# A two-layer metaformer in float32: the first state of each scan chunk, the last inverse transforms, and where VectorE's reductions stand

## The chip, the cores and the metric

The kernel runs on one core of one Trainium2 chip, in one launch. The metric is the device time of that launch in microseconds (us), and the median of several runs is compared. PE is the tensor engine, DVE the vector engine, ACT the scalar engine, POOL GpSimd, and SP the engine whose queue issues nearly all DMAs here.

## The reference, cut to what matters

The input is `x[4, 64, 64, 128]`: four images of 4096 tokens with 128 channels, all in float32. Layer 0 is a selective scan in four directions (`K = 4`, 256 inner channels, 16 states) and a mixture of 64 experts; layer 1 is a sum over rows and columns and a long convolution with 16 spectral filters. The parts that the change touches:

```python
def step(h, xs):                      # layer 0, conv: 4096 steps for each batch and direction
    ut, dt, bt, ct = xs
    dA = jnp.exp(dt[..., None] * A)
    h = dA * h + (dt * ut)[..., None] * bt[:, :, None, :]
    y = jnp.einsum('bkdn,bkn->bkd', h, ct)
    return (h, y)
...
logits = jnp.einsum('bsd,ed->bse', x, gate_w) + gate_b        # layer 0, experts
probs = jax.nn.softmax(logits, axis=1)                        # over the 4096 tokens
vals, idx = jax.lax.top_k(probs.transpose(0, 2, 1), K)
...
message_m = jnp.sum(inputs, axis=2)                           # layer 1, conv
message_k = jnp.sum(inputs, axis=1)
...
Uf_p = jnp.fft.rfft(u, n=n, axis=1)                           # layer 1, filters
U_plus = jnp.fft.irfft(Vf[None, :, :, None] * Uf_p[:, :, None, :], n=n, axis=1)[:, :sl]
...
x = x + _L1_conv_ref(_ln_c(x), ...)
t = _to_tokens(x)
t = t + _L1_ffn_ref(_ln_t(t), ...)
```

## The kernel before, in words

**The scan loop.** The main loop (`for s in range(-5, total + 2)`) walks over 2048 steps: 4 batches, 4 directions, 8 chunks of 512 tokens (`SC`), 16 states each. One step does one state of one chunk, for 2 x 128 channels and 512 tokens, on all engines, each at its own distance. SP loads `bc` (the rows B and C of that state, spread over 128 partitions) five steps ahead, L1435. ACT computes `da = exp(delta * A)` three steps ahead in two halves, L1445. DVE multiplies `db = du * B` into PSUM (L1473) and runs two scans `h = da * h + db` (L1479), one for each half of the channels. POOL stores the last column for the next chunk (`hst`, L1488) and multiplies by C one step behind (L1489). PE transposes and sums into `y` two steps behind, L1515. There are six `hh` buffers and five `da`; `db`, `du` and `y` have one PSUM buffer each.

**delta*x.** `step_sizes` prepares the next chunk in pieces, one a step: `dts` is projected, ACT and POOL make the softplus `dl`, and the last piece is POOL's product `dx = dl * xc` (L1377), in SBUF with one buffer. At state 15 of a chunk `into_psum` has ACT copy `dx` to `du` in PSUM in two halves (L1426). Every `db` of the next chunk reads `du`, the first one included.

**Side work.** The rest of the network is dealt between the scan's instructions: `beside(b)` is a generator whose pieces give their weight, and `deal` draws pieces until as much weight is made as is due. `WEIGHT` holds the total weight of each batch's side work, and so the pace. [...] a side instruction stands in its engine's queue between those of the scan. `pipelined(n, *stages)` staggers the stages of a piece of work: in each step the latest stage is written first, and a `None` is a step's distance. `LAG` (5.0) is a pause.

**Maxima and row sums.** `experts_and_sums` norms the tokens, transposes them (`turn`), and projects the gate's logits on PE (`logits`); ACT moves them to `pT` (L742), and DVE takes the maximum of each group of 512 tokens (L756), as the next stage of the same pipeline. Later, in the same manner, ACT (through `evict`, L257) writes transposed tokens to `xT`, DVE sums their rows (`mm`, L969), and then their columns (`mk`, L976).

**The tail.** After the scans, `side["tail"]` is set and eight PSUM banks are open. `convolve` runs the filters' matmuls (L1166, L1187) for the groups of frequencies that are left; a second generator runs beside it, first the last batch's experts and sums, then `back()`, the inverse transforms of batches 1 and 2. `ratio` sets how much filter work is drawn for each unit of it. PE's order is fixed by dependencies that `behind` adds. Last comes `from_slots(B - 1)`: it loads the products of the filters (`zb`, L1246) and the residual tokens (`xr` from `x3_d`, L1252), multiplies by the inverse transform on PE (`gi_ps`, L1259), scales on ACT (`iv`, L1261), adds on POOL (L1269) and stores (L1272), eight groups in a pipeline of five stages. Batch 0's inverse transforms run earlier, beside the scans of the last batch.

Of the kernel before, what the change touches and what calls it, by code (L numbers as in the profile page):

```python
# [10 lines left out]
F32 = mybir.dt.float32  # L11
# [20 lines left out]


FIRST = 1
WEIGHT = (1346.0, 2070.0, 1989.0, 2042.0)

BUSY = (2, 3)

# [40 lines left out]
def kernel(  # L79
# [137 lines left out]
    def evict_soon(work):  # L217
        if side["deals"]:
            soon.append(work)
        else:  # L220
            work()
# [113 lines left out]
    def transposed(dst, src, n, name):  # L335

        ps = bank([P, n, P], name)
        for q in range(n):
            nc.tensor.transpose(ps[:, q, :], src[:, q, :], ident)
        evict_soon(lambda: evict(dst, ps.rearrange("c q p -> c (q p)")))  # L340
# [374 lines left out]
    def experts_and_sums(b):  # L715

        with tc.tile_pool(name="mk", bufs=1) as kp:
# [3 lines left out]
            with tc.tile_pool(name="ga", bufs=2) as gp:  # L721
                tt = gp.tile([P, NBLK, C], F32, name="tt", bufs=1)
                mx8 = gp.tile([E, 8], F32, name="mx8", bufs=1)
                st, tT = {}, {}

                def t4(g):
                    return tt[:, 4 * g : 4 * g + 4, :]

                def gs(g):
                    return slice(512 * g, 512 * (g + 1))  # L730

                def sums(g):
                    st[g] = norm_sums(gp, t4(g), 4, C, eps5)

                def turn(g):
                    tT[g] = gp.tile([P, 512], F32, name="tT")
                    transposed(tT[g], t4(g), 4, "tt_ps")

                def logits(g):
                    ps = bank([E, 512], "lg_ps")  # L740
                    nc.tensor.matmul(ps, gw, tT[g], start=True, stop=True)
                    nc.scalar.activation(pT[:, gs(g)], ps, AF.Identity, bias=gb)  # L742

                yield from pipelined(
                    8,
                    (0.4, lambda g: nc.sync.dma_start(t4(g), tiles(x1_d[b], g))),
                    (3.0, sums),
                    (1.2, lambda g: norm_refine(gp, st[g], 4, C, 1e-5)),
                    None,
                    (1.2, lambda g: norm_apply(t4(g), t4(g), st[g], 4)),  # L750
                    None,
                    (1.0, turn),
                    (1.0, logits),
                    (
                        0.6,
                        lambda g: nc.vector.reduce_max(  # L756
                            mx8[:, g : g + 1], pT[:, gs(g)], axis=AX.X
                        ),
                    ),
                )  # L760

                nmx = gp.tile([E, 1], F32, name="nmx", bufs=1)
                nc.vector.reduce_max(nmx, mx8, axis=AX.X)
                nc.vector.tensor_scalar(nmx, nmx, -1.0, None, ALU.mult)
                s8 = gp.tile([E, 8], F32, name="s8", bufs=1)
                for g in range(8):
                    nc.scalar.activation(
                        pT[:, gs(g)], pT[:, gs(g)], AF.Exp, bias=nmx, accum_out=s8[:, g : g + 1]
                    )
                    yield 0.8  # L770
                yield LAG
                ssum = gp.tile([E, 1], F32, name="ssum", bufs=1)
                nc.vector.reduce_sum(ssum, s8, axis=AX.X)
                nc.vector.reciprocal(ssum, ssum)
                yield 1.0
                for g in range(8):
                    nc.scalar.activation(pT[:, gs(g)], pT[:, gs(g)], AF.Identity, scale=ssum)
                    yield 0.8
                yield LAG
                top = gp.tile([E, TOPK], F32, name="top", bufs=1)  # L780
                nc.vector.max(top, pT)
                yield 1.0
                rest = gp.tile([E, L], F32, name="rest", bufs=1)
                nc.vector.match_replace(rest, top, pT, 0.0)
                yield 1.0
                for g in range(8):
                    nc.gpsimd.tensor_sub(pT[:, gs(g)], pT[:, gs(g)], rest[:, gs(g)])
                    yield 1.2
                yield LAG
                po = bank([P, E], "po_ps")  # L790
                pk = {}

                def turn_back(g):
                    ps = bank([P, 8, E], "pk_ps")
                    for q in range(8):
                        t0 = (8 * g + q) * P
                        nc.tensor.transpose(ps[:, q, :], pT[:, t0 : t0 + P], ident[0:E, 0:E])
                    pk[g] = gp.tile([P, 8, E], F32, name="pk")
                    evict(pk[g], ps)

                def pool(g):
                    for q in range(8):
                        nc.tensor.matmul(
                            po,
                            tt[:, 8 * g + q, :],
                            pk[g][:, q, :],
                            start=(g == 0 and q == 0),
                            stop=(g == 3 and q == 7),
                        )

                yield from pipelined(4, (1.5, turn_back), (3.0, pool))
                evict(pooled, po)
                yield 1.0
                yield LAG
# [106 lines left out]
            with tc.tile_pool(name="l1", bufs=2) as lp:  # L921
# [4 lines left out]
                with tc.tile_pool(name="l1a", bufs=2) as la:  # L926
# [25 lines left out]
                    def apply(g):  # L952
# [11 lines left out]
                        (1.2, apply),  # L964
                        None,
                        (1.0, lambda g: transposed(xT[:, gs(g)], xn[g], 4, "xn_ps")),
                        (
                            0.6,
                            lambda g: nc.vector.reduce_sum(  # L969
# [3 lines left out]
                            ),  # L973
                        ),
                    )
                nc.vector.reduce_sum(  # L976
                    mk[:, 0, :], xT.rearrange("p (r w) -> p w r", w=W), axis=AX.X
                )
# [254 lines left out]

    def from_slots(b):

        with tc.tile_pool(name="gi", bufs=3) as gp:
            zb, xr, iv = {}, {}, {}

            def here(g):
                t0 = 2 * (BS - 4 * (g + 1))  # L1240
                return slice(t0, t0 + 8)

            def load(g):
                zb[g] = gp.tile([P, 4, 2, C], F32, name="zb")
                for r in range(2):
                    nc.sync.dma_start(  # L1246
                        zb[g][r * NQ : (r + 1) * NQ], zd[b][:, r, 4 * g : 4 * g + 4]
                    )

            def turn(g):  # L1250
                xr[g] = gp.tile([NB, 4, 2, C], F32, name="xr3", bufs=5)
                nc.sync.dma_start(  # L1252
                    xr[g].rearrange("j t a c -> j (t a) c"),
                    x3_d[b].rearrange("(j t) c -> j t c", j=NB)[:, here(g), :],
                )
                iv[g] = gp.tile([NB, 4, 2, C], F32, name="iv", bufs=4)
                for a in range(2):
                    ps = bank([NB, 4, C], "gi_ps")
                    nc.tensor.matmul(ps, gi_t, zb[g][:, :, a, :], start=True, stop=True)  # L1259
                    evict_soon(  # L1260
                        lambda ps=ps, a=a: nc.scalar.activation(  # L1261
                            iv[g][:, :, a, :], ps, AF.Identity, scale=wpj[0:NB, :]
                        )
                    )

            def add(g):

                for t in range(4):
                    nc.gpsimd.tensor_add(xr[g][:, t], xr[g][:, t], iv[g][:, 3 - t])  # L1269

            def put(g):
                nc.sync.dma_start(  # L1272
                    out[b].rearrange("(j t) c -> j t c", j=NB)[:, here(g), :],
                    xr[g].rearrange("j t a c -> j (t a) c"),
                )

            yield from pipelined(BS // 4, (0.7, load), (2.5, turn), None, (3.0, add), (0.5, put))

    def run(pieces):
        for _ in pieces:  # L1280
            tick()
        flush()
# [21 lines left out]
    with ExitStack() as c0:  # L1304
# [123 lines left out]
        for s in range(-5, total + 2):  # L1428
# [23 lines left out]
            if 0 <= s < total:  # L1452
# [17 lines left out]
                        next(sizes[i + 1][3], None)  # L1470
                hhs[s] = pb.tile([P, 2, SC], F32, name="hh", bufs=6)
                db = bps.tile([P, 2, SC], F32, name="db")
                nc.vector.tensor_mul(db, dus[i], bcs[s][:, 0:1, :].to_broadcast([P, 2, SC]))  # L1473
                for h in range(2):
                    init = 0.0 if step == 0 else hsts[i][:, h, n : n + 1]
                    o, d0, d1 = hhs[s][:, h, :], das[s][:, h, :], db[:, h, :]
# [76 lines left out]
    def first_stages():  # L1553
        yield from after_scans(B - 1)
        yield from experts_and_sums(B - 1)
        yield from to_slots(B - 1)

    def back():
        for b in range(1, B - 1):
            yield from from_slots(b)  # L1560

    last = len(all_groups) - NQ // 4
    with tc.tile_pool(name="cv_tail", bufs=2) as cp:

        for stages, groups, ratio in (
            (first_stages(), all_groups[BESIDE * (B - 1) : last], 3.2),
            (back(), all_groups[last:], 18.0),
        ):
            filtered = convolve(groups, cp)
            due = made = 0.0  # L1570
# [10 lines left out]
                start = len(traced)  # L1581
            run(filtered)
            behind(start, True)
    run(from_slots(B - 1))
    side["pool"].close()


# [72 lines left out]
```

## Time and profile before

| what | value |
|---|---|
| median of 3 runs | 11044.66 us (11032.29 to 11044.76) |
| the profiled execution | 11042.23 us, its span 11040.4 us, mean TensorE clock 0.864 |
| busy over the span | PE 79%, DVE 74%, ACT 57%, POOL 61% |
| L1489 POOL `hh<-hh,bc` | 2048 x 2358 ns |
| L1479 DVE `hh<-da,hst,db` (and `hh<-da,db`) | 3584 x 1267 ns (512 x 1208 ns) |
| L1473 DVE `db<-du,bc` | 2048 x 1232 ns |
| L1426 ACT `du<-dx` | 256 x 590 ns |
| L756 and L969 DVE `mx<-pT`, `mm<-xT` | 32 each, median 678 ns |
| L976 DVE `mk<-xT` | 4, median 7125 ns |
| L1261 ACT `iv<-gi_ps`, L1269 POOL `xr<-xr,iv` | 64 x 681 ns, 128 x 719 ns |

The times come from one profiled execution. Busy time counts only what an engine works on; a wait shows as idle time in front of an instruction, with the instruction that ended it named behind an arrow. The share of an engine over the whole span mixes stages with different limits, so the stages are read one by one. [...]

### The profile page before, as it was taken

The page shows a single profiled execution, that of the slowest core. Times are in us where ns is not written, and L with a number is a line of the kernel's source. Part 1 is how long each engine was busy: PE and PEld are TensorE (multiplying, and loading weights), DVE is VectorE, ACT ScalarE, POOL GpSimd, SP SyncE. Part 2 cuts the span into 40 slices and gives each one's busy share as a digit, 9 for nine tenths or more (in the row PEclk, how much of TensorE's full clock was granted, in tenths as well). Part 3 has the DMA queues.
Part 4 walks back from the last instruction along what each step waited for, and adds up shares of the span by engine and source line. Part 5 has one row for each costly group of instructions (what it writes and reads, how often), then busy time and mean ns, then how long its engine had stood idle before and what let it go on. Part 6 is the DMA issues. An engine that isn't in the chain of part 4 may idle for free. (4 is left out here: it accounts for less than half of the span.)

```text
span 11040.4 us, 119413 instructions
## 1 busy us (share of the span) xinstructions
PE 8697.3 (79%) x35936; PEld 4908.8 (44%) x35936; DVE 8146.2 (74%) x7046; ACT 6261.4 (57%) x12203; POOL 6771.4 (61%) x6198
## 2 busy tenths in 40 slices
PE   6787777657777777778776677687677789999999
PEld 2444444334464444445543334455344444355443
DVE  0888989987897999989988899798799922222222
ACT  4767676757567565675755556657565634134222
POOL 1777777877777878777777777677788711001001
PEclk9788888768887888878878888798888899999999
DMA  2455656657666666657565566475766664554555
GB/s 95 166 201 171 206 177 211 205 183 223 212 197 194 196 181 197 206 178 253 171 190 173 173 183 213 155 271 163 205 190 194 186 159 118 147 136 105 134 134 122
DMA packets 901466, 1980.29 MB, mean 179 GB/s; under 512 B 101562, under 2 KB 415578, under 8 KB 899290
## 3 DMA queue, kind: packets, MB, share of 16 engines
q1 hardware_dynamic: 900826, 1972.65, 59.2%
q8 instruction: 293, 4.80, 0.2%
q14 instruction: 347, 2.84, 0.1%
HBM read 1766.77 MB, written 205.52 MB: 179 GB/s over the span
## 5 line engine op out<-in xcount | busy, mean ns | idle before, releaser
L1489 POOL TENSOR_TENSOR hh<-hh,bc 128x1024 f32<-128x1024 f32 x2048 | 4827.9, 2358 | 419.5 <-DVE hh L1479 181.2
L1479 DVE TENSOR_TENSOR_SCAN hh<-da,hst,db 128x512 f32<-128x512 f32 x3584 | 4393.2, 1267 | 547.7 <-PE y L1515 165.7
L1445 ACT ACTIVATE da<-dl,aneg 128x512 f32<-128x512 f32 x4096 | 2773.3, 717 | 2018.1 <-DVE hh L1479 1946.7
L1515 PE MATMUL y<-ident,hh 128*128 128x128 f32 x16384 | 2655.8, 311 | 644.9 <-POOL hh L1489 538.5
L1515 PEld LDWEIGHTS y<-ident,hh 128*128 128x128 f32 x16384 | 2204.1, 161 | 2025.0 <-issue 1076.1
L1473 DVE TENSOR_TENSOR db<-du,bc 128x1024 f32<-128x1024 f32 x2048 | 2523.6, 1232 | 576.1 <-ACT du L1426 486.4
L1166 PE MATMUL cv_ps<-slab,us 64*128 64x512 f32 x4096 | 1169.4, 678 | 513.0 <-ACT y L257 276.5
L257 ACT COPY y<-cv_ps 128x512 f32<-128x512 f32 (+1 forms) x1024 | 754.9, 741 | 666.8 <-PE cv_ps L1166 636.6
L1488 POOL COPY hst<-hh 128x2 f32<-128x2 f32 x1792 | 336.4, 188 | 1237.8 <-DVE hh L1479 1111.3
L1187 PE MATMUL zq_ps<-y,me 128*128 128x512 f32 x2048 | 992.4, 604 | 44.8 <-ACT y L257 43.4
L1187 PE MATMUL zq_ps<-y,mo 128*128 128x512 f32 x2048 | 977.7, 601 | 0.0
L255 DVE COPY y<-cv_ps 128x512 f32<-128x512 f32 x640 | 441.9, 691 | 568.0 <-PE cv_ps L1166 550.3
L1166 PEld LDWEIGHTS cv_ps<-slab,us 64*128 64x128 f32 x4096 | 400.0, 203 | 963.1 <-ACT y L257 364.8
L1203 POOL TENSOR_TENSOR zt<-zt,zt 128x512 f32<-128x512 f32 x64 | 81.1, 1267 | 1082.7 <-DVE zt L255 571.4
L1479 DVE TENSOR_TENSOR_SCAN hh<-da,db 128x512 f32<-128x512 f32 x512 | 597.0, 1208 | 50.4 <-PE y L1515 14.0
L411 PE MATMUL cv_ps<-xh,diag 128*128 128x512 f32 x1152 | 529.1, 602 | 9.8 <-ACT dl L1370 6.9
L1187 PEld LDWEIGHTS zq_ps<-y,me 128*128 128x128 f32 x2048 | 348.7, 191 | 375.6 <-issue 261.3
L1187 PEld LDWEIGHTS zq_ps<-y,mo 128*128 128x128 f32 x2048 | 359.5, 192 | 317.1 <-issue 315.1
L1335 PE MATMUL dt_ps<-dts,dtw 8*128 8x512 f32 x512 | 336.0, 769 | 147.0 <-ACT sg_v L353 42.2
L255 DVE COPY zt<-zq_ps 128x512 f32<-128x512 f32 x40 | 27.7, 691 | 549.6 <-PE zq_ps L1187 549.6
L1361 POOL TENSOR_TENSOR ex<-ex,dx 128x1024 f32<-128x1024 f32 x128 | 302.4, 2363 | 159.3 <-ACT dx L1358 149.6
L317 POOL TENSOR_SCALAR no_a<-no_v 128x2 f32<-128x2 f32 (+1 forms) x224 | 43.0, 192 | 528.1 <-ACT no_sq L306 516.0
(232 smaller groups left out, 9290.4 us busy)
## 6 DMA issues: line engine op xcount, KB each, us to landing
bc<-bc_d SPq DMA_DIRECT2D x2048, 512.0 KB
slab<-hd SPq DMA_DIRECT2D x1024, 256.0 KB
xc<-xc_d SPq DMA_DIRECT2D x128, 512.0 KB
y_d<-ys SPq DMA_DIRECT2D x128, 512.0 KB
w1t<-in_w_dram SPq DMA_DIRECT2D x128, 512.0 KB
w2t<-in_w_dram SPq DMA_DIRECT2D x256, 256.0 KB
xc_x<-xc_d SPq DMA_DIRECT2D x64, 512.0 KB
yk<-y_d SPq DMA_DIRECT2D x128, 256.0 KB
```

The lines of the kernel that those rows point to most:

```text
L255: nc.vector.tensor_copy(dst, src)
L257: nc.scalar.copy(dst, src)
L411: nc.tensor.matmul(ps, diag[:, h, t, :], xh[:, 8 * g + dy : 8 * g + dy + 8, dx : dx + W], start=(t == 0), stop=(t == 8),)
L1166: nc.tensor.matmul(pq[q].rearrange("p (r k t) -> p r k t", r=2, t=BS), us[b, G][rows, p, a if e == 0 else 1 - a, :], slab[i][rows, p, :, : ...
L1187: nc.tensor.matmul(z, (me, mo)[e][:, KQ * kq + k, :], ys[e][:, :, :, :, k, :].rearrange("p a q r t -> p (a q r) t"), start=(e == 0 and k = ...
L1335: nc.tensor.matmul(ps, dtw[:, k, h * P : (h + 1) * P], dts, start=True, stop=True)
L1445: i_act = nc.scalar.activation(das[t][:, h, :], sizes[t // N][0][:, h, :], AF.Exp, scale=aneg[:, tk, h, t % N : t % N + 1],)
L1473: nc.vector.tensor_mul(db, dus[i], bcs[s][:, 0:1, :].to_broadcast([P, 2, SC]))
L1479: i_dve = nc.vector.tensor_tensor_scan(o, d0, d1, init, ALU.mult, ALU.add)
L1488: nc.gpsimd.tensor_copy(hsts[t // N][:, :, t % N], hhs[t][:, :, last])
L1489: i_pool = nc.gpsimd.tensor_mul(hhs[t], hhs[t], bcs.pop(t)[:, 1:2, :].to_broadcast([P, 2, SC]))
L1515: i_pe = nc.tensor.matmul(ys[c][:, q, h, :], hhs[t][:, h, q * P : (q + 1) * P], ident, is_transpose=True, start=(n == 0 and k > 0 and q % ...
```

## The change

Three edits, and two numbers that follow from them.

1. In the scan loop, the `db` of state 0 reads `dx` in SBUF (`sizes[i][1]`) in place of `du` in PSUM. The copies to `du` stay, and states 1 to 15 read `du`.
2. In `experts_and_sums`, a `None` stands in front of the maxima and in front of the row sums, and a `LAG` behind each of the two pipelines. `WEIGHT` of batches 1 to 3 grows by 10.
3. In the tail, `from_slots` has DVE read the inverse transform from PSUM, scale it and add the residual in one instruction (`scalar_tensor_tensor`) in place of ACT's scaling and POOL's addition; the stage in between and the addition's stage fall away, and the residual tokens (`load_x`) of all eight groups are loaded first, into eight buffers. For the last batch these loads are drawn at the end of `back()`, while the filters still run; the rest of it runs behind the filters as before. `ratio` of `back()` goes from 18 to 28.

```diff
--- before.py
+++ after.py
@@ -32,7 +32,7 @@
 
 
 FIRST = 1
-WEIGHT = (1346.0, 2070.0, 1989.0, 2042.0)
+WEIGHT = (1346.0, 2080.0, 1999.0, 2052.0)
 
 BUSY = (2, 3)
 
@@ -751,6 +751,7 @@
                     None,
                     (1.0, turn),
                     (1.0, logits),
+                    None,
                     (
                         0.6,
                         lambda g: nc.vector.reduce_max(
@@ -758,6 +759,7 @@
                         ),
                     ),
                 )
+                yield LAG
 
                 nmx = gp.tile([E, 1], F32, name="nmx", bufs=1)
                 nc.vector.reduce_max(nmx, mx8, axis=AX.X)
@@ -964,6 +966,7 @@
                         (1.2, apply),
                         None,
                         (1.0, lambda g: transposed(xT[:, gs(g)], xn[g], 4, "xn_ps")),
+                        None,
                         (
                             0.6,
                             lambda g: nc.vector.reduce_sum(
@@ -973,6 +976,7 @@
                             ),
                         ),
                     )
+                yield LAG
                 nc.vector.reduce_sum(
                     mk[:, 0, :], xT.rearrange("p (r w) -> p w r", w=W), axis=AX.X
                 )
@@ -1233,12 +1237,20 @@
 
     def from_slots(b):
 
-        with tc.tile_pool(name="gi", bufs=3) as gp:
+        tail = side["tail"]
+        with tc.tile_pool(name="gi", bufs=4 if tail else 3) as gp:
             zb, xr, iv = {}, {}, {}
 
             def here(g):
                 t0 = 2 * (BS - 4 * (g + 1))
                 return slice(t0, t0 + 8)
+
+            def load_x(g):
+                xr[g] = gp.tile([NB, 4, 2, C], F32, name="xr3", bufs=8 if tail else 5)
+                nc.sync.dma_start(
+                    xr[g].rearrange("j t a c -> j (t a) c"),
+                    x3_d[b].rearrange("(j t) c -> j t c", j=NB)[:, here(g), :],
+                )
 
             def load(g):
                 zb[g] = gp.tile([P, 4, 2, C], F32, name="zb")
@@ -1248,15 +1260,23 @@
                     )
 
             def turn(g):
-                xr[g] = gp.tile([NB, 4, 2, C], F32, name="xr3", bufs=5)
-                nc.sync.dma_start(
-                    xr[g].rearrange("j t a c -> j (t a) c"),
-                    x3_d[b].rearrange("(j t) c -> j t c", j=NB)[:, here(g), :],
-                )
-                iv[g] = gp.tile([NB, 4, 2, C], F32, name="iv", bufs=4)
+                if not tail:
+                    load_x(g)
+                    iv[g] = gp.tile([NB, 4, 2, C], F32, name="iv", bufs=4)
                 for a in range(2):
                     ps = bank([NB, 4, C], "gi_ps")
                     nc.tensor.matmul(ps, gi_t, zb[g][:, :, a, :], start=True, stop=True)
+                    if tail:
+
+                        nc.vector.scalar_tensor_tensor(
+                            xr[g][:, :, a, :],
+                            ps[:, ::-1, :],
+                            wpj[0:NB, :],
+                            xr[g][:, :, a, :],
+                            ALU.mult,
+                            ALU.add,
+                        )
+                        continue
                     evict_soon(
                         lambda ps=ps, a=a: nc.scalar.activation(
                             iv[g][:, :, a, :], ps, AF.Identity, scale=wpj[0:NB, :]
@@ -1274,6 +1294,12 @@
                     xr[g].rearrange("j t a c -> j (t a) c"),
                 )
 
+            if tail:
+                for g in range(BS // 4):
+                    load_x(g)
+                    yield 0.5
+                yield from pipelined(BS // 4, (0.7, load), (2.5, turn), (0.5, put))
+                return
             yield from pipelined(BS // 4, (0.7, load), (2.5, turn), None, (3.0, add), (0.5, put))
 
     def run(pieces):
@@ -1470,7 +1496,9 @@
                         next(sizes[i + 1][3], None)
                 hhs[s] = pb.tile([P, 2, SC], F32, name="hh", bufs=6)
                 db = bps.tile([P, 2, SC], F32, name="db")
-                nc.vector.tensor_mul(db, dus[i], bcs[s][:, 0:1, :].to_broadcast([P, 2, SC]))
+
+                src = sizes[i][1] if n == 0 else dus[i]
+                nc.vector.tensor_mul(db, src, bcs[s][:, 0:1, :].to_broadcast([P, 2, SC]))
                 for h in range(2):
                     init = 0.0 if step == 0 else hsts[i][:, h, n : n + 1]
                     o, d0, d1 = hhs[s][:, h, :], das[s][:, h, :], db[:, h, :]
@@ -1555,16 +1583,21 @@
         yield from experts_and_sums(B - 1)
         yield from to_slots(B - 1)
 
+    ends = from_slots(B - 1)
+
     def back():
         for b in range(1, B - 1):
             yield from from_slots(b)
 
+        for g in range(BS // 4):
+            yield next(ends)
+
     last = len(all_groups) - NQ // 4
     with tc.tile_pool(name="cv_tail", bufs=2) as cp:
 
         for stages, groups, ratio in (
             (first_stages(), all_groups[BESIDE * (B - 1) : last], 3.2),
-            (back(), all_groups[last:], 18.0),
+            (back(), all_groups[last:], 28.0),
         ):
             filtered = convolve(groups, cp)
             due = made = 0.0
@@ -1581,7 +1614,7 @@
                 start = len(traced)
             run(filtered)
             behind(start, True)
-    run(from_slots(B - 1))
+        run(ends)
     side["pool"].close()
```

## The prediction

> **What bounds the kernel now.** I read the page's slices first, then busy time by stretch, then VectorE's waits inside the first stretch. The slices show two regimes: VectorE (DVE) is nine tenths busy for 31 slices, then TensorE (PE) is.
>
> ```profile
> PE   6787777657777777778776677687677789999999
> DVE  0888989987897999989988899798799922222222
> ```
>
> The stretches (columns: length, then busy time and instructions of PE, weight loads, DVE, ACT, POOL, then clock and DMA) put the border at 8866 us:
>
> ```profile
> 297.00:8866.00 8569.00, 6374.86 (x28311) 3874.30 (x28312) 7599.45 (x6240) 5436.69 (x10260) 6510.21 (x5627) 0.83 0.62 194
> 8866.00:10995.00 2129.00, 2098.45 (x7139) 946.22 (x7137) 541.58 (x779) 678.98 (x1608) 201.89 (x458) 0.99 0.53 132
> 10995.00:11041.00 46.00, 20.71 (x36) 5.08 (x36) 0.69 (x1) 11.50 (x17) 23.22 (x33) 0.78 0.74 188
> ```
>
> Scan stage: 2048 steps in 8569 us, 4.18 us each, of which DVE works 3.71. Its 970 us of idle time is partly the short gap before each instruction; the rest are named waits, and only those can be saved. In the filter tail PE idles 31 us of 2129, so nothing on DVE, ACT or POOL pays there. The last 46 us are a chain of their own. DVE's waits in the scan stage (total, times, longest):
>
> ```profile
> DVE db L1473 <- ACT du L1426: 486.4, 57, 286.9
> DVE hh L1479 <- PE y L1515: 179.7, 55, 14.6
> DVE hh L1479 <- ACT da L1445: 66.9, 32, 7.4
> DVE mx L756 <- ACT pT L742: 54.1, 16, 6.6
> DVE mm L969 <- ACT xT L257: 19.3, 6, 5.5
> ```
>
> The 286.9 is the start-up, before the first scan. The other 56 waits on `du`, 199.5 us, fall at chunk starts: ACT's two copies of `dx` into PSUM stand behind side work in ACT's queue, and DVE waits for them. The last two lines are the maxima and row sums waiting for ACT's output.
>
> **What the Trainium skill says.** SBUF — State Buffer, Who interferes with whom: a VectorE instruction with two SBUF inputs contends with a GpSimd instruction that reads SBUF; the port is locked for the whole instruction and the later one blocks. That bears on the first part: `dx` and `bc` both lie in SBUF, `du` did not. The trace agrees. Timeline rows (start, length), from the few small two-input operations of the filter weights:
>
> ```profile
> 2277.16 0.15 DVE L631 TENSOR_TENSOR wt<-hard,soft 128x4 f32<-128x4 f32 x1
> 2277.52 2.35 POOL L1489 TENSOR_TENSOR hh<-hh,bc 128x1024 f32<-128x1024 f32 x1
> 2278.37 1.52 DVE L632 TENSOR_TENSOR wt<-wt,soft 128x4 f32<-128x4 f32 x1
> ...
> 2283.49 0.21 DVE L636 TENSOR_TENSOR wseg<-wseg,wt 128x1 f32<-128x1 f32 x1
> 2283.51 0.18 POOL L1488 COPY hst<-hh 128x2 f32<-128x2 f32 x1
> 2283.77 2.34 POOL L1489 TENSOR_TENSOR hh<-hh,bc 128x1024 f32<-128x1024 f32 x1
> ```
>
> The same form takes 0.15 us with POOL idle and 1.52 us when it meets a POOL product: it ends at 2279.89, just after the product at 2279.87. The last three rows show a DVE operation held by the short `hst` copy (until 2283.69) and let through before the product starts at 2283.77. VectorE: DVE Perf Modes, The TRN2 errata, prices an fp32 tensor_tensor at (N+151)/0.96 ns: 1224 ns for 1024 elements. The trace has 1232 with `du` in PSUM, so unblocked the new form costs the same.
>
> **Part 1: first state from SBUF.** Nothing is removed: ACT still copies `du`, for states 1 to 15. What moves is when DVE needs it. I went through the 127 chunk starts after the first one by one in the timeline.
> 1. At 58 of them DVE idles longer than the usual 0.09 us: 196 us together.
> 2. Now it must wait only for POOL's `dx` product, which ended before the last scan at 121 of 127. The six late ones keep 22 us: 174 us of waits go.
> 3. State 1 still needs `du`, but DVE comes there one state later, 3.77 us (1.23 + 2 x 1.27). 18 of the waits are longer, and the excess comes back at state 1: 121 us are left.
> 4. The lock. In quiet starts POOL's `hst` copy begins 0.064 us after the scan and ends at 0.252, while `db` would start at 0.091: 0.16 us lost. Where POOL is inside another operation its remainder is lost, up to 2.36 us. Summed over the starts: 50 us. Put through steps 2 and 3 again, the gain falls to **79 us**.
>
> Start-up adds 2.7 us (`dx` ends at 294.3, the first `db` started at 297.2). Bounds: 121 us if DVE wins every race; a loss if POOL wins twice (below). The other side of the lock: POOL is held about 1.2 us at each of 128 starts, some 150 us, with the products, PE's transposes and the `hh` buffers queued behind it. POOL idles 2059 us of this stage (8569 - 6510), so I charge nothing by itself, but it lowers what is kept.
>
> **Part 2: reductions one pipeline step later.** 48 reductions in this stage, 22 of which waited, 73.4 us. In the built programs' order I counted, in scan steps, how far each stands on DVE behind its producer on ACT: the 24 maxima stood 57.5 steps behind in sum and now stand 75.5, mostly by 1 to 2.5 steps at the end of each pipeline, where they waited. At 4.18 us a step I took from each wait its own shift: 20 of 54.1 us and 2.5 of 19.3 remain. **Gain 50 us**, bounds 25 (half the shift, since ACT is often behind) and 73. The two LAG pauses add 10 units to some 2070, which the weights repeat: side work is dealt 0.5% denser, no time. In the tail these waits are covered by PE.
>
> **Part 3: last inverse transforms.** For batches 1 and 2 inside the filter tail, DVE gains 32 reads of PSUM at about 0.69 us (nearest row: `y<-cv_ps`, 691 ns for 512 columns), 22 us on an engine busy 542 of 2129; ACT and POOL lose work that PE covered. Zero; were a read to hold up the `y` evictions queued behind it, at most 1 us for each of 32 (-5 to +30). For batch 3 the eight `x3` loads, 0.59 us each on SP, move in front of the last filters: they pass slab loads with DMA at 0.53 and PE waiting 3.8 us for slabs in the whole tail. Zero. The last 46 us then change. Rows of their end now:
>
> ```profile
> 11022.64 1.29 SPq L1246 DMA_DIRECT2D zb<-zd  x2
> 11031.11 1.90 PE L1259 MATMUL gi_ps<-zb,gi_t 128*64 128x512 f32 x4 [1.80 <-DMA zb<-zd]
> 11032.27 1.46 ACT L1261 ACTIVATE iv<-gi_ps,wpj 64x512 f32<-64x512 f32 x2 [2.24 <-PE gi_ps L1259]
> 11033.86 2.76 POOL L1269 TENSOR_TENSOR xr<-xr,iv 64x256 f32<-64x256 f32 x4 [0.27 <-POOL xr L1269]
> ```
>
> From 11001 to 11031 DMA is full at some 240 GB/s, with 4.2 MB of `zb`, 2.1 of `xr` and the first outputs. Without the 2.1 MB it ends 8.7 us earlier; ACT's 1.46 plus POOL's 2.76 become DVE's last 0.7: 3.5 us. SP stands in order and now has stores between the loads: 1 to 2 us back. **Gain 11 us**, bounds 3 and 16.
>
> **The sum.** Of parts 1 and 2, 79 + 3 + 50 = 132 us. Not all will be kept: while DVE waited, the others caught up, and the waits for PE's `y` (179.7) and ACT's `da` (66.9) will grow. The trace can't show how much; I take three quarters (bounds half and all): 99. With the tail, 110. The profiled execution took 11042.2 us (span 11040.4 and 1.8 around it): 10932. The median of the runs, 11044.7, is 2.4 above it: **10935 us**.
>
> **The rivals.**
> - *All kept, races won.* 121 + 3 + 73 + 15 = 212: 10833. For it: DVE is the busiest engine by 1089 us. Against: 1.2 us of POOL time is taken at each start, and `hst` starts 27 ns ahead.
> - *Given back.* The saved waits turn into waits for `y` and `da`, since ACT's backlog also delays POOL's `no_a` (71.9 us of waits on `no_sq`) and with it the products. Only the tail stays: 11033. Against: 55 such waits in 2048 steps, with six `hh` buffers.
> - *Slower: the port is lost twice.* If POOL's product, queued right behind the `hst` copy, takes the port again before `db`, each start loses 2.4 us more wherever the next POOL operation follows within 0.25 us. The same walk gives 244 us of holding and a loss of 110 in place of the 79. With reductions and tail as above, it is 11045 + 110 - 3 - 50 - 11 = 11091. It decides at a mean holding above some 1.6 us a start, against 0.4 in the forecast. For it: `db` needs the port for 1.2 us, the probes in the trace for 0.1. Against: the rows at 2283, and 2278, where POOL's next addition began at 2279.83, yet the probe got through at 2279.89.
> - *The reductions do not move.* The order says they do; the bound of 25 covers it.
>
> **How the numbers follow.** Chances: forecast 0.64, all kept 0.10, given back 0.12, port lost twice 0.14. 0.2% is 22 us, about what a measurement here can tell from no change (the three runs span 12). Faster 0.76, with a small part of "given back"; same 0.10; slower 0.14. The forecast's own range, from its bounds, is 10890 to 10985; the 8 in 10 reach to the other cases: 10860 to 11060.
>
> **What would show it.** Step 1: a group `db<-dx,bc` x128 with a mean near 1.6 us (1.23 + 0.4), and the wait on `du` under 60 us, at state 1. A mean above 2.8 is the slower rival; 1.23 means no lock. Part 2: waits of `mx` and `mm` under 30 us together. Part 3: from the last filter matmul to the end about 35 us, not 45. Kept share: waits for `y` and `da`, now 247 us, growing by no more than 35; if they grow by 100, the gain was given back. The prediction is wrong if the scan stage is shorter by under 50 us or by over 150.

## The result and the profile after

The changed kernel takes 10990.1 us (median of 5 runs, 10987.4 to 10994.6) against 11044.7 for the kernel before (5 runs). The ratio is 0.9953, with a 95% interval of 0.9942 to 0.9964: 54.6 us are gained, half of the 110 that the prediction forecast. The profiled execution took 10988.0 us, its span is 10986.2 us and its mean TensorE clock 0.861.

The slices of the kernel after (tenths busy in 40 slices) look as they did: DVE is busy for 31 slices, then PE.

```profile
PE   6787777657876777768777677687777799999999
DVE  0898989987998999989989899798799922222322
```

The stretches of the kernel after, cut at the first `db`, at the last scan and at the last filter matmul (columns as before: length, then PE, weight loads, DVE, ACT, POOL, clock, DMA):

```profile
294.00:8797.00 8503.00, 6380.65 (x28302) 3880.49 (x28303) 7637.15 (x6240) 5439.07 (x10266) 6625.06 (x5627) 0.83 0.62 195
8797.00:10940.00 2143.00, 2107.49 (x7148) 949.56 (x7146) 565.60 (x813) 658.13 (x1576) 160.32 (x395) 0.99 0.53 132
10940.00:10987.00 47.00, 22.58 (x36) 5.78 (x36) 12.55 (x17) 0.59 (x1) 1.26 (x1) 0.71 0.55 140
```

The scan stage became shorter and the filter tail longer. Cut exactly at those instructions, the scans end at 8797.0 us instead of 8861.9 (3.0 of it from the start-up, whose first `db` starts at 294.2). The filter tail then takes 2142.9 us instead of 2133.0, and the end 46.3 instead of 45.5: -64.9 + 9.9 + 0.8 = -54.2 us. DVE's waits in the scan stage (columns: total, times, longest):

```profile
DVE db L1501 <- POOL dx L1403: 318.0, 9, 284.2
DVE hh L1507 <- PE y L1543: 205.6, 79, 14.7
DVE hh L1507 <- ACT da L1471: 92.7, 31, 8.3
DVE db L1501 <- ACT du L1452: 64.2, 17, 11.1
...
DVE mx L757 <- ACT pT L742: 17.2, 8, 4.8
```

Without the start-up's 284.2, the waits on `dx` and `du` are 33.8 + 64.2 = 98 us, where `du` alone had 199.5. The maxima and row sums wait 26.2 us in place of 73.4 (`mm`, 9.0, stands further down). But `y` and `da` rose from 247 to 298. The groups of the page (busy, mean ns | idle before) for the new form and for POOL's `hst` copy:

```profile
L1516 POOL COPY hst<-hh 128x2 f32<-128x2 f32 x1792 | 392.0, 219 | 1090.9 <-DVE hh L1507 960.6
...
L1501 DVE TENSOR_TENSOR db<-dx,bc 128x1024 f32<-128x1024 f32 x128 | 196.8, 1537 | 326.2 <-POOL dx L1403 318.0
```

The mean of 1537 ns is not typical: 98 of the 128 took under 1.26 us, and the other 30 hold the whole excess over 1232 ns, 39 us. The reader sees why in two timelines of the kernel after (start, length). First a quiet chunk start:

```profile
1009.24 0.19 POOL L1516 COPY hst<-hh 128x2 f32<-128x2 f32 x1
1009.27 1.24 DVE L1501 TENSOR_TENSOR db<-dx,bc 128x1024 f32<-128x1024 f32 x1
...
1009.50 3.21 POOL L1517 TENSOR_TENSOR hh<-hh,bc 128x1024 f32<-128x1024 f32 x1
```

Then one where POOL is inside side work:

```profile
1972.03 1.27 POOL L500 TENSOR_TENSOR sg_v<-sg_v,sg_e 128x512 f32<-128x512 f32 x1
...
1972.17 2.22 DVE L1501 TENSOR_TENSOR db<-dx,bc 128x1024 f32<-128x1024 f32 x1
...
1973.24 1.18 POOL L1516 COPY hst<-hh 128x2 f32<-128x2 f32 x1
```

In the first, DVE pays 0.01 us, although `hst` is recorded as starting first; the product behind `hst`, which takes 2.36 us elsewhere, takes 3.21, because it stands until `db` is done. In the second `db` waits some 1 us until the side product ends at 1973.30, and then `hst` waits for `db`. The lock is there, and mostly POOL stands in it: 54 products and 54 copies were held, 105 us together, and side operations of POOL some 16 us more.

### The profile page after: what moved, and what is told of

Its sections match the earlier page's. It is cut to its first block, busy times and chain, and to the rows that moved or that the text cites. A ratio compares the mean times of both kernels' runs of the same rounds, so it can differ in the third digit from the quotient of the medians.

```text
span 10986.2 us, 119383 instructions
## 1 busy us (share of the span) xinstructions
PE 8713.2 (79%) x35936; PEld 4918.8 (45%) x35936; DVE 8219.8 (75%) x7094; ACT 6229.3 (57%) x12156; POOL 6822.5 (62%) x6102
## 5 line engine op out<-in xcount | busy, mean ns | idle before, releaser
L1501 DVE TENSOR_TENSOR db<-du,bc 128x1024 f32<-128x1024 f32 x1920 | 2365.6, 1232 | 153.4 <-ACT du L1452 64.2
L1516 POOL COPY hst<-hh 128x2 f32<-128x2 f32 x1792 | 392.0, 219 | 1090.9 <-DVE hh L1507 960.6
L1501 DVE TENSOR_TENSOR db<-dx,bc 128x1024 f32<-128x1024 f32 x128 | 196.8, 1537 | 326.2 <-POOL dx L1403 318.0
```

The lines of the kernel that those rows point to most:

```text
L1501: nc.vector.tensor_mul(db, src, bcs[s][:, 0:1, :].to_broadcast([P, 2, SC]))
L1516: nc.gpsimd.tensor_copy(hsts[t // N][:, :, t % N], hhs[t][:, :, last])
```

## The experiments

Theory: the first part brings what was forecast, and the second gives some of it back, by pauses that move side work. Rival: the first part brings less, since the lock or POOL's backlog takes it. The stage lengths below are read as above; "before" is 8564.7 us for the scan stage, 2133.0 for the tail, 45.5 for the end.

**The parts alone.** Part 1 alone:

```diff
-nc.vector.tensor_mul(db, dus[i], bcs[s][:, 0:1, :].to_broadcast([P, 2, SC]))
+src = sizes[i][1] if n == 0 else dus[i]
+nc.vector.tensor_mul(db, src, bcs[s][:, 0:1, :].to_broadcast([P, 2, SC]))
```

> The kernel before with part 1 alone: state 0 of each chunk multiplies dx from SBUF. Both theories: start-up 3 us earlier, the waits on du and dx at chunk starts fall from 199 us to about 100, the 128 new products last about 1.54 us in the mean (39 us more than before in all). Backlog theory (what is saved comes back because ACT's and POOL's side work is late anyway): DVE's waits for y and da grow by 20 to 35 us, the scan stage ends 30 to 45 us earlier, ratio about 0.9965. Port theory (POOL, held at each start, makes y late): these waits grow by the full 50 us seen with all parts, the scan stage ends 15 us earlier or less, ratio about 0.999. All kept: 65 us earlier, ratio 0.994. The tail is untouched: within 3 us of before.

Measured: 10966.6 us, ratio 0.9928 (0.9915 to 0.9942); 76 us faster than before and 23 faster than the whole change. The scan stage took 8491.9 us, 73 less. DVE's waits there, part 1 alone:

```profile
DVE db L1475 <- POOL dx L1377: 308.4, 6, 286.1
DVE hh L1481 <- PE y L1517: 188.1, 63, 17.1
DVE hh L1481 <- ACT da L1445: 92.6, 39, 7.4
DVE db L1475 <- ACT du L1426: 53.7, 14, 9.8
...
DVE mx L756 <- ACT pT L742: 31.4, 12, 7.5
```

`dx` keeps 22.3 us and `du` 53.7, so 123 us of waits went. The lock cost 45 (mean 1581 ns). The rest, 78, is what the walk through the chunk starts gave, and the stage is 73 us shorter, more than even "all kept" expected. The port theory falls. But the 73 are not simply 78 less a little. `y` and `da` took 34 us back, as the backlog theory expected, and the maxima and row sums waited 32 us less (41.7 in place of 73.4), which nobody had expected: their code is the same. The one edited line changed the built order elsewhere too: counted as in the prediction, the 24 maxima of this stage stood 57.5 scan steps in sum behind ACT's `pT` and now stand 68.5.

Part 2 alone (both `None`, both `LAG`, and `WEIGHT`, as in the diff of the change):

> The kernel before with part 2 alone: the maxima and row sums one pipeline step later, the two pauses, the weights. Waits of mx and mm in the scan stage fall from 73 to about 26 us. Backlog theory: a third to a half of the 47 us comes back as waits for y and da, the scan stage ends 25 to 35 us earlier. Port theory: nothing is given back, since no port is taken, and it ends 45 us earlier. The filter tail: if the pauses in the last batch's sums are what made it 10 us longer, it is 7 to 10 us longer here too and the ratio is about 0.998; if DVE's new reads did that, it is as long as before and the ratio is 0.996 to 0.997.

Measured: 11078.9 us, ratio 1.0032 (1.0020 to 1.0045): 36 us slower. The scan stage took 8589.1 us (+24), the tail 2142.6 (+10). The waits of maxima and row sums did fall, from 73.4 to 49.3 us, but `du` rose from 199 to 229, `y` from 180 to 200 and `da` from 67 to 94. Both theories had expected a gain.

Part 3 alone (all edits of `from_slots` and of `back()`):

> The kernel before with part 3 alone: last inverse transforms on DVE, residual tokens loaded first, ratio 28. Scan stage as before within 3 us. If DVE's new reads hold up the filters, the filter tail is 10 us longer; if the pauses of part 2 did it, within 3 us of before. From the last filter matmul to the end: 45 to 47 us as with all parts, if SP's order of loads and stores sets it; 35 if what was seen with all parts was a matter of that run. Ratio 1.000 within 0.0005 (1.001 if the reads cost).

Measured: 11039.2 us, 0.9995 (0.9987 to 1.0003), no difference. Tail 2132.0 us, end 45.2. The 32 reads by DVE inside the tail are free, as forecast; the gain of 11 us at the end did not come.

**The lock, magnified.** States 1 to 4 read `dx`, when it has long been there, and state 0 reads `du` as before:

```diff
+src = sizes[i][1] if 1 <= n <= 4 else dus[i]
```

> The kernel before with states 1 to 4 of each chunk, in place of state 0, multiplying dx from SBUF: 512 products with two SBUF inputs, and no wait on du is avoided (state 0 still reads du). It prices the port by itself. Backlog theory: only the direct hold, 0.3 us for each, 155 us at most, and less where DVE would have waited anyway: 80 to 155 us slower, ratio 1.007 to 1.014. Port theory: POOL, held four times a chunk, makes y late and DVE wait for it: 250 us slower or more, ratio 1.023 or above. No price: 1.000.

Measured: 11131.3 us, 1.0081 (1.0067 to 1.0095). DVE's group with `dx`, by line (busy, mean | idle), in this kernel:

```profile
L1475 DVE TENSOR_TENSOR db<-dx,bc 128x1024 f32<-128x1024 f32 x512 | 694.9, 1357 | 31.5 <-DMA bc<-bc_d 10.2
```

and POOL's copy:

```profile
L1490 POOL COPY hst<-hh 128x2 f32<-128x2 f32 x1792 | 714.0, 398 | 879.1 <-DVE hh L1481 795.6
```

DVE lost 0.125 us an instruction, 64 us in all; POOL was held some 480 us (361 copies and 114 products). The stage grew by 96 us: 64 from the lock and 32 by waits (`y` 20 and `du` 18 more, others fewer). So the price of holding POOL is not nothing, but small. And the rival by which the port is lost twice does not describe the usual case: 54 of the 512 started while an `hst` copy ran with a product queued right behind it, and none of them lost more than 0.03 us. Yet the port can be lost more than once. In part 1 alone one `db` of 128 met side additions of POOL:

```profile
7788.02 2.76 POOL L1269 TENSOR_TENSOR xr<-xr,iv 64x256 f32<-64x256 f32 x4
...
7789.73 6.73 DVE L1475 TENSOR_TENSOR db<-dx,bc 128x1024 f32<-128x1024 f32 x1
...
7790.75 4.62 POOL L1491 TENSOR_TENSOR hh<-hh,bc 128x1024 f32<-128x1024 f32 x2
```

Two products that are recorded as starting 1 us and more after `db` ran through at their usual 2.3 us each, and `db` ended 1.1 us behind them. This one cost 5.5 of the 45 us. The magnified lock has one `db` like it (3.95 us), the whole change none (3.38 at most). What sets these apart isn't known.

**Why part 2 loses.** Its pieces, taken apart. The pauses and the weights without the moved reductions:

```diff
-WEIGHT = (1346.0, 2070.0, 1989.0, 2042.0)
+WEIGHT = (1346.0, 2080.0, 1999.0, 2052.0)
...
+yield LAG          # behind the maxima
...
+yield LAG          # behind the row sums
```

> The kernel before with the two pauses and the weights of part 2, without the stages in between. Phase theory (the pauses move all later side work by 10 units, some 36 us, against the chunk starts, and other pieces now meet them): the stretches that got worse with part 2 get worse here too (last third of batch 2 and chunks 12 to 15 of batch 3, 10 to 20 us each), the maxima still wait about 50 us, ratio 1.003 to 1.006, the filter tail 8 to 10 us longer. Place theory (the later reductions themselves cost): scan stage within 8 us of before, ratio about 1.001 from the tail alone.

Measured: 11085.5 us, 1.0036 (1.0023 to 1.0050); stage 8593.2, tail 2146.4.

The moved reductions without pauses (the two `None` alone, old weights):

> The kernel before with the stage in front of the maxima and row sums, without the pauses and with the old weights. Phase theory: the waits of mx and mm fall to 25 to 35 us, nothing else moves by more than 10 us, ratio 0.996 to 0.998, tail within 3 us of before. Place theory: the scan stage is 15 to 30 us longer, ratio 1.0015 to 1.003.

Measured: 11042.7 us, 1.0000 (0.9992 to 1.0008); stage 8560.3, tail 2133.5. The maxima and row sums waited 55 us instead of 73, and nothing came of it, which neither theory had expected. (By the same count this edit moves the maxima by one step only, from 57.5 to 58.5, so it says nothing of a larger move.) The pauses carry the loss. What do they do? The same shift put elsewhere answers it: two pauses at the start of the side work of batches 1 to 3, with the reductions and everything between them as before.

```diff
         else:
+            yield LAG
+            yield LAG
             yield from after_scans(b - 1)
```

> The kernel before with two pauses at the start of the side work of batches 1 to 3, and the weights of part 2: the reductions stand as before, all the side work of these batches comes 10 units later. Phase theory: batch 0 takes the same time within 1 us, and in the other batches single groups of four chunks move by 5 to 20 us either way, though no work and no dependency of the reductions has changed; the sum can have either sign, at most 40 us. Place theory: no group moves by more than 3 us, ratio 1.000. The filter tail does not see this edit: within 3 us.

Measured: 11094.9 us, 1.0046 (1.0034 to 1.0059); stage 8612.0, tail 2133.8; the stage lost 47 us, and at most 40 were expected. So it isn't the reductions' place that costs, but that side work comes later against the chunks. The weight of a batch, 2070, is spent over 31 chunks of some 67 us, so a unit is about 1 us and the two pauses about 10 us, a sixth of a chunk. (Where the expectations put the 10 units at some 36 us, that was a slip of mine.) The delay doesn't last: with the larger weight a batch's work is dealt faster, and at the batch's end little of it is left. By ACT's order, at 4.18 us a step, side work stands on average 4 us later in the first group of the next table and 7 us later in the second, in all three kernels. Time of four chunks together, less that of the kernel before, in us:

| chunks | before | part 2 | pauses | shift | `None` | part 3 |
|---|---|---|---|---|---|---|
| batch 2, 16 to 19 | 257.4 | +17.9 | +19.0 | +17.2 | -3.1 | 0.0 |
| batch 3, 12 to 15 | 295.0 | +13.9 | +13.5 | +16.2 | +3.6 | +0.4 |

In these two groups the three kernels with the shift lose about the same. In chunks 0 to 3 of batch 2, where side work comes 11 us later in the shifted kernel and at the same place in the other two, the shifted one loses 11.5 us and the others 3.1 and 0.8. A delay need not cost, though: in chunks 0 to 3 of batch 3 it is 10 us in the shifted kernel, which loses nothing there. All three have the larger weights; no run has these alone. Kernels whose scan stage is the same program, such as part 3 alone, stay mostly within 1.4 us of before in such groups, so these differences are not noise. DVE's busy time in both groups is unchanged. In the second group its waits are, in the kernel before,

```profile
DVE hh L1479 <- PE y L1515: 17.4, 3, 14.6
DVE hh L1479 <- POOL dx L1377: 15.5, 1, 15.5
```

in part 2 alone,

```profile
DVE hh L1483 <- PE y L1519: 39.2, 6, 14.2
...
DVE hh L1483 <- ACT du L1430: 5.8, 1, 5.8
```

and in the shifted kernel

```profile
DVE hh L1481 <- PE y L1517: 41.7, 7, 13.9
...
DVE hh L1481 <- ACT du L1428: 5.8, 1, 5.8
```

The last two have the same stalls. The 15.5 of before is not gone in them: at the same place stands a stall of 14 us that is listed under `y`. New are two of 5.8 us, one on `y` and one on `du`, and smaller ones. In the first group, from its first `db` to the next group's, the `du` waits grew from 10.4 us to 25.7 in part 2 alone and 25.0 in the shifted kernel. ACT's evictions of the filters stand among the `du` copies there, but in the kernel before they do so too; why they cost more when they come 4 us later is open. With part 1 this group is no slower than before (-3.5 us, and -0.5 in the whole change), since `db` no longer waits for `du` there; the second group is (+17.1 and +25.6).

**The whole without part 2, and the end.** Parts 1 and 3 with the old weights. In the last batch all 16 `zb` loads are issued first, into eight buffers:

```diff
-with tc.tile_pool(name="gi", bufs=4 if tail else 3) as gp:
+with tc.tile_pool(name="gi", bufs=8 if tail else 3) as gp:
...
+if b == B - 1:
+    for g in range(BS // 4):
+        load(g)
+    yield from pipelined(BS // 4, (2.5, turn), (0.5, put))
+    return
```

> Parts 1 and 3 of the change without part 2, and for the last batch all sixteen loads of the filters' products issued before the first store, with eight buffers in place of four. If SP's order is what kept the end at 46 us: from the last filter matmul to the end 36 to 40 us. If the transfers themselves do: 44 to 46. The scan stage as with part 1 alone (8492 us within 5), the filter tail as before. In all 10955 to 10960 us, ratio about 0.992, faster than all parts together by 30 us.

Measured: 10947.0 us, 0.9914 (0.9900 to 0.9927); stage 8492.4, tail 2132.1, end 32.4, shorter than the 36 to 40 expected. The end explains itself in SP's queue. In the kernel after (timeline: start, time over which they are issued):

```profile
10945.60 4.28 SPq L1258 DMA_DIRECT2D zb<-zd  x7
10954.65 3.46 SPq L1292 DMA_DIRECT2D out_dram<-xr  x2
10958.15 0.60 SPq L1258 DMA_DIRECT2D zb<-zd  x1
...
10965.40 5.48 SPq L1292 DMA_DIRECT2D out_dram<-xr  x2
10970.97 1.19 SPq L1258 DMA_DIRECT2D zb<-zd  x2
```

and with all loads first:

```profile
10924.35 11.58 SPq L1254 DMA_DIRECT2D zb<-zd  x16
10936.65 10.75 SPq L1288 DMA_DIRECT2D out_dram<-xr  x8
```

A store waits in SP's queue until DVE has made its data, and holds the loads behind it: between 10949.9 and 10958.2 no `zb` was issued. DVE then waits for PE, and PE for `zb`. The run changed the number of buffers together with the order, but in the kernel after SP waited mostly for DVE's data and hardly for a buffer that PE still read:

```profile
SPq L1292 <- DVE xr L1271: 22.1, 7, 5.0
...
SPq L1258 <- PE gi_ps L1268: 0.6, 1, 0.6
```

The same with the two `None` (no pauses):

> Parts 1 and 3 with all loads first, and part 2's stage in front of the reductions, but without its pauses and with the old weights. Phase theory: the reductions' own place is worth what it removes, here the 43 us of mx and mm waits that are left, down to some 30, and the rest moves by chance: scan stage 8485 to 8500 us, the filter tail 2132 us, ratio 0.990 to 0.992. Place theory: 20 us or more slower than parts 1 and 3 alone, ratio 0.993 or above.

Measured: 10947.9 us, 0.9916 (0.9903 to 0.9930): no gain with part 1 in place either, though the maxima and row sums waited 35 us instead of 43.

A second state read from SBUF, as `du` still made state 1 wait 54 us:

```diff
-src = sizes[i][1] if n == 0 else dus[i]
+src = sizes[i][1] if n <= 1 else dus[i]
```

> Parts 1 and 3 with all loads first, with states 0 and 1 of each chunk reading dx. The du wait, 55 us with one state, is needed one state later: at most 15 us of it left. The second product meets the port as the states 1 to 4 did in the run that priced it, 0.13 us each, 16 us. Net 20 to 25 us faster than with one state if DVE keeps it, ratio 0.9895; 0.9914 if it comes back as waits for y and da.

Measured: 10975.4 us, 0.9942 (0.9929 to 0.9954), 28 us slower than with one state: a miss. The `du` waits fell to 18.7 us, 36 less, but the lock took 71 us instead of 45, `y` 216 instead of 188 and `da` 100 instead of 90.

Last, half of the shift, one pause of 5 units at the start of the side work of batches 1 to 3, on top of parts 1 and 3:

```diff
+yield LAG
 yield from after_scans(b - 1)
```

> Parts 1 and 3 with all loads first, and one pause of 5 units, half of what part 2 adds, at the start of the side work of batches 1 to 3. A unit of weight is about one us of scan time (2070 units over 31 chunks of some 67 us). Phase theory: with part 1 in place most of what the phase does to the du waits is hidden, so what is left shows in chunks 12 to 15 of batch 3 (waits for y), 0 to 15 us longer, and other groups move by up to 10 us: ratio 0.990 to 0.9935. If the phase no longer matters with part 1: no group of four chunks moves by more than 3 us, ratio 0.9914.

Measured: 10930.5 us, 0.9901 (0.9886 to 0.9916), outside what was expected and on the good side: the fastest version here, 107 us under the kernel before in the same runs (11037.8). Its interval overlaps with those of the two kernels above that have no shift, so the last 12 us (by the ratios; 17 against the kernel with the two `None`, measured beside it) are likely and not certain. Against the kernel without the shift, four chunks at a time, it gains up to 10 us in some groups (14.5 over batch 1's chunks 0 to 7) and loses 13 in another (batch 2, 0 to 3). Its `du` waits are 41 us in place of 54 and its `y` waits 220 in place of 188; a wait of 20 us of a scan, listed under POOL's `dx`, is gone, and many small waits are shorter. A shift moves losses about; 5 units happened to be good and 10 bad. Other values were not tried, so where the best phase lies is open.

**The tail.** It takes 2143 to 2146 us in the three kernels with pauses behind the reductions, and 2131 to 2136 in the nine others of the experiments, the shifted one among them, whose pauses are beside the scans only. So those inside the tail, where the last batch's reductions run, cost about 10 us there. In the kernel after, PE's timeline shows a wait:

```profile
10132.06 4.46 PE L1191 MATMUL zq_ps<-y,mo 128*128 128x512 f32 x10
10139.75 5.64 PE L1106 MATMUL fu_ps<-ub,fu_t 64*128 64x512 f32 x7 [3.24 <-DMA ub<-u_d]
```

and the stretches around it (the clock is the column after POOL) a slower PE behind it:

```profile
10139.00:10150.00 11.00, 10.25 (x26) 4.93 (x27) 3.30 (x5) 2.91 (x5) 0.00 (x0) 0.69 0.60 157
10128.00:10139.00 11.00, 8.52 (x31) 4.29 (x30) 0.69 (x1) 1.32 (x3) 1.45 (x2) 1.00 0.46 125
```

The records give half clock for 6.83 us from 10140.4. The two other kernels with pauses in the tail have the same wait (3.1 us in each) and the same 6.83 us at this place, and none of the kernels without has either there. The Trainium skill (TensorE: Matmul & The Clock Gate, What's actually happening) says that an idle window of about 3.4 us puts PE at half its clock. The trace agrees only in part, since shorter recorded pauses go with it too: in the tail of the kernel before, pauses of 2.81, 1.63 and 2.26 us (ending at 9220, 9238 and 10280) are each followed by half clock for 3.41 us. Over the tail the time below full clock grew from 28.8 to 36.1 us: 3.2 of waiting and half of the 7.3 make 7 of the 10 us. The other 3 are open.

## Why the prediction was half right

*Direction and bound.* DVE's waits in the scan stage set the time, and cutting them paid. Both hold for part 1; the 18 us cut by the two `None` alone paid nothing.

*Part 1, 79 us, start-up 3.* Right, with some luck. Alone it freed 123 us of waits (forecast 121 after the excess at state 1), paid 45 for the lock (forecast 42 on the path) and shortened the stage by 73. In these 73 stand 32 us that the forecast didn't have, the shorter waits of the maxima and row sums; they made up for the 34 us that `y` and `da` took back. (The start-up's 3 us are true only on average: the first `db` starts at 294.2 to 297.4 in the kernels with `dx` and at 296.5 to 300.8 in those with `du`.) The lock's mean had the right size for a partly wrong reason. The forecast charged 0.16 us at quiet starts for `hst`; the trace shows 0.01 there, 98 starts of 128, and 1.3 us at each of the other 30. The Trainium skill's rule (SBUF — State Buffer, Who interferes with whom) holds as to the whole instruction. But the recorded start doesn't tell who has the port: a copy of two elements, recorded 27 ns ahead, did not hold `db`, and two products recorded as starting later than a `db` went ahead of it.

*"I charge nothing" for POOL's holding.* Nearly right. Forecast 150 us of holding, measured some 120; in the magnified lock 480 us of it went with 32 us more of DVE's waits.

*Part 2, 50 us: the step that failed.* The waits of maxima and row sums fell to 26 us in the whole change, forecast 22.5, but not by part 2: part 1 alone left 41.7 and part 2 alone 49.3. So part 2 removed 24 us of waits by itself and 15 behind part 1, not 50. The prediction read the moved order from the program with all parts: of its 18 steps 11 come with part 1 alone, and 9 with part 2 alone. Above all, "side work is dealt 0.5% denser, no time" failed. The weights keep the pace, not the phase: behind the pauses side work comes later against the chunk starts, by 4 to 7 us where the loss stands, and part 2 alone costs 24 us in the scan stage and 10 in the tail. And "in the tail covered by PE" was judged from the reductions' waits, not from the pauses, which delay what PE needs later. Without the pauses the `None` are worth nothing measurable (1.0000), since other waits took the place of those 18 us (`du` and `y` 7 us more each).

*"Three quarters" kept.* One share for both parts hid that they differ: of part 1 alone the stage got about nine tenths, with the help told above, and of part 2 nothing. `y` and `da` grew by 52 us in the whole change (forecast up to 35), by 34 with part 1 alone. Behind the parts' sum, then: 99 forecast for stage and start-up, 65 measured; 74 with part 1 alone.

*Part 3, 11 us.* The tail's zero was right (2132.0 us against 2133.0 before). At the end, "1 to 2 us back" for SP's order was mis-sized: it ate the whole gain. With the loads first the end is 32.4 us, so the order and the four buffers that it went with cost 13 to 14, more than the 11. DVE's instruction itself took 0.74 us, forecast 0.7.

*The rivals.* The port lost twice is not the rule, as the magnified lock shows, though single products did lose it more than once. "Given back" is half true: the phase takes part 2's gain and more, and part 1 alone gives 34 us back in waits for `y` and `da`. Whether POOL's backlog is behind these is not shown.

## What to carry to other kernels

A wait that is shortened counts only if nothing else is moved to shorten it: when an edit adds a pause or a piece to work that is dealt in order, test the bare shift at another place before crediting or blaming the edit. Compare the built order as well: one changed operand moved reductions that nobody had edited. In a queue that runs in order, issue all loads that have a buffer before the first store that waits for computed data. On a port that two engines share, magnify the conflict fourfold and read both engines' groups: the loser's duration grows, and its start does not tell who lost.

## What was not expected of the hardware

A `db` of 1.23 us that meets a 0.19 us `hst` copy, recorded 27 ns ahead, took 1.24 us; the product behind the copy was held for 0.85. In part 1 alone a `db` was held for 5.5 us while POOL ran two products that are recorded as starting after it. When `db` is recorded ahead of `hst` the copy takes 1.2 us instead of 0.19. DVE's addition of a scaled 64x512 tile from PSUM takes 0.74 us, against 0.68 for ACT's scaling and two POOL additions of 0.72 each. And side work shifted by 5 or 10 units, of some 2070 a batch, moved the time of the whole kernel by some -0.13% (ratio 0.9914 to 0.9901, the intervals overlapping) and +0.46%.
